# Layer 1's sixteen experts placed ahead of the shared expert in a four-layer kernel

## The chip, the cores and the metric

The kernel runs on one core of a Trainium2 chip. The metric is device time in microseconds for one launch; lower is better. A core has a matrix engine (PE, with its weight loads shown apart as PEld), a vector engine (DVE), a scalar engine (ACT), a general engine (POOL) and a queue engine (SP). Each works through its own instructions in the order in which they were laid down, and they meet through semaphores. SP issues the ordinary transfers of this kernel, POOL the indirect ones (rows scattered or gathered by a list of positions).

## The reference, cut to what matters

The program is a stack of four layers over x of shape 4 x 1024 x 128. Each layer has a mixing step and a feed-forward step, each added to x and followed by a layer norm. The change lies in layer 1's feed-forward step: 16 experts of width 128, of which every token takes four, and a shared expert of width 256 that every token takes.

```python
x = _layernorm(x + _L0_attn_ref(x, ...)); x = _layernorm(x + _L0_ffn_ref(x, ...))
x = _layernorm(x + _L1_attn_ref(x, ...)); x = _layernorm(x + _L1_ffn_ref(x, ...))
x = _layernorm(x + _L2_attn_ref(x, ...)); x = _layernorm(x + _L2_ffn_ref(x, ...))
x = _layernorm(x + _L3_attn_ref(x, ...)); x = _layernorm(x + _L3_ffn_ref(x, ...))

def _L1_ffn_ref(hidden_states, ...):          # layer 1's feed-forward step
    topk_idx, tw = _route(x, router_w, bias)  # 4 of 16 experts for each token
    combine = (one_hot(topk_idx, E) * tw[..., None]).sum(1)
    h = einsum('td,edf->etf', x, gate_w); u = einsum('td,edf->etf', x, up_w)
    y = einsum('etf,efd->etd', silu(h) * u, down_w)
    routed = einsum('etd,te->td', y, combine)
    sh = silu(x @ sh_gate_w) * (x @ sh_up_w) @ sh_down_w
    return routed + sh
```

Routed part and shared part are summed into the same rows of x before the norm, so they may be computed in either order.

## The kernel before, in words

All arithmetic is float32. x lies in on-chip memory as 32 tiles of 128 tokens; eight tiles are a quarter of the sequence positions. The first half is quarters 0 and 1 (part `a`), the second half quarters 2 and 3 (part `r` in layer 1). A transposed copy, `xT`, feeds the matrix multiplications.

Layer 1's experts are reached through lists in device memory. `spread` (L1305) scatters each row of x four times into the list `l1ra`, sorted by expert: 64 indirect transfers on POOL. `l1_experts` (`small_experts`, L1713 and following) works through the list in 18 groups of four tiles: SP loads a group's rows `xg` (L1336), PE turns them, multiplies by the gate and up weights (`gu`), ACT and DVE form `hg` (L1743, L1744), PE turns and multiplies by the down weights (`yp`), and SP stores the result `yg` to the list `l1ya` (L1762). Two further groups stand in a branch that is taken only when the lists are longer than that. `l1_close` then calls `collect`: POOL gathers the four rows of each token tile from `l1ya` into a tile `yt` (64 indirect transfers again, into a ring of five tiles), and DVE adds them with their weights to x (L1396, four instructions a tile). After eight tiles it norms the quarter, saves it (`xsave`) and turns it into `xT`.

`l1_shared` is the shared expert: for each of four blocks of 512 tokens four multiplications of 128x512 (`pg`, `pu`), SiLU on ACT (L743), a product on DVE (L744, `hs`), eight multiplications `py`, and one DVE addition to x (L830). Its weights are three loads of 128 KB (`swg`, `swu`, `swd`).

The second half runs as a companion: `side` is `l0_ffn` of quarters 2 and 3 (a quantised linear layer, DVE and POOL lines L487 to L544) and then `l1_attn` of quarters 2 and 3 (a state recurrence: L649 multiplies, L653 scans, L671 and L672 multiply back, L680 adds to x, then a norm by nine small DVE instructions and the eight of L212). `l2_weights` merges layer 2's weights in 24 steps, which start from the load `ld<-in_l_big` (1536 KB) and store through `we` (L1448, L1450).

The order is set by Python generators. `mix(main, side, pace)` advances the side by planned costs while the main generator is laid down; `chain` runs generators one after another, `abreast` side by side. The instructions are then ordered for each engine by a scheduler with priorities, and buffers of a pool that is closed are handed to the next pool, so that a load into a new pool waits for the last reader of the old one. The lines around the change are these:

```python
side = self.chain(self.l0_ffn((2, 3), True), self.l1_attn((2, 3), True))
self.run(self.mix(self.chain(self.l1_shared(a), self.l1_experts(a, wall)), side, 2.0, False))
self.run(self.mix(self.abreast(self.l2_weights(), side), self.l1_close(a, yp)))
```

After them come `l2_attn(0)`, which needs both quarters of the first half closed, and everything else.

Of the kernel before, what the change touches and what calls it, by code (L numbers as in the profile page):

```python
# [74 lines left out]
class Kernel:  # L75
# [737 lines left out]
    def l1_shared(self, part):  # L813

        nc, x = self.nc, self.x
        with ExitStack() as ctx:
            cp = self.pool(ctx, "l1sc" + part.name)
            hp = self.pool(ctx, "l1sh" + part.name, 2)
            ps = self.pool(ctx, "l1sp" + part.name, 2, space=PSUM)
            swg = self.load(cp, self.ins["l1_swg"])  # L820
            swu = self.load(cp, self.ins["l1_swu"])
            swd = self.load(cp, self.ins["l1_swd"])
            for blk in range(part.t0 // 4, (part.t0 + part.nt) // 4):
                h = self.tile(hp, [P, 2, BLK], "hs")
                for c in range(2):
                    f = slice(c * P, (c + 1) * P)
                    self.glu(ps, hp, h[:, c, :], swg[:, f], swu[:, f], blk)
                py = self.down(ps, h, swd, 2)
                tl = slice(blk * 4, blk * 4 + 4)
                nc.vector.tensor_tensor(x[:, tl, :], py, x[:, tl, :], ALU.add)  # L830
                yield (5.5,)

    def l1_close(self, part, yp):

        nc, x = self.nc, self.x
        for q in range(part.q0, part.q0 + part.nq):
            yield from self.collect("l1", part, K1, yp, (q - part.q0) * QT, QT)
            self.norm(self.quarter(q))
            tl = slice(q * QT, (q + 1) * QT)
            nc.sync.dma_start(out=self.xsave[:, tl, :], in_=x[:, tl, :])  # L840
            yield (6.0,)
            for g in range(2):
                self.turned(self.side, q * QT + g * 4, tag="s")
                yield (1.5,)
# [1037 lines left out]
    def all(self):  # L1882
        a, rest = self.first, self.rest
        b, c = rest
        r = self.both[1]
        a2, m2, n2 = self.by_rows
        with ExitStack() as ctx:
            lgp = self.pool(ctx, "l2lg")
            self.l2_lg = self.tile(lgp, [P, NT, E2], "lg")
            with ExitStack() as early:  # L1890

                self.l0_setup(early)
                self.l2_wr = self.load(lgp, self.ins["l2_wr"])
                self.run(self.l0_attn((0, 1)))
                self.l1_setup()
                self.l2_setup()
                self.zero_lists("l1")
                self.run(self.l0_ffn((0, 1)))
                self.run(self.l1_attn((0, 1)))

                self.run(self.l1_route(a))
                self.run(self.mix(self.l0_attn((2, 3), True), self.spread("l1", a, K1)))
                self.zero_lists("l2", "l3")
                with ExitStack() as c2:
                    wall = self.l1_wall(c2)
                    yp = self.pool(c2, "l1ya", 5, right=True)
                    side = self.chain(self.l0_ffn((2, 3), True), self.l1_attn((2, 3), True))
                    self.run(self.mix(self.chain(self.l1_shared(a), self.l1_experts(a, wall)), side, 2.0, False))
                    self.run(self.mix(self.abreast(self.l2_weights(), side), self.l1_close(a, yp)))
            with ExitStack() as c2:  # L1910
                wall = self.l1_wall(c2)
                self.run(self.mix(self.l2_attn(0), self.chain(self.l1_route(r), self.spread("l1", r, K1))))
                wall2 = self.l2_wall(c2)
                yp = self.pool(c2, "l1yr", 5, right=True)
                self.run(self.mix(self.chain(self.l1_experts(r, wall), self.l1_shared(r)), self.routed(a2)))
                self.run(self.mix(self.l2_experts(a2, wall2), self.l1_close(r, yp)))
            listed = lambda name: lambda: name in self.listed
            on = self.served(
                self.chain(self.rows_in(a2), self.onward(a, True)),
                (lambda: self.rows_done >= B + 2, self.routed(m2)),  # L1920
                (lambda: self.rows_done == 2 * B, self.routed(n2)),
            )
            self.run(self.mix(self.l2_attn(1), on, drain=False))
            with ExitStack() as c3:
                with ExitStack() as c2:
                    wall = self.l2_wall(c2)
                    self.press(on, listed("l2m"))
                    self.run(self.mix(self.l2_experts(m2, wall), on, drain=False))
                    self.press(on, lambda: {"l2n", "routed l3a"} <= self.listed)
                    sw, wall3 = self.l3_wall(c3, True)  # L1930
                    on = self.chain(on, self.rows_in(m2))
                    self.run(self.mix(self.l2_experts(n2, wall), on, drain=False))
                self.press(on, listed("l3a"))
                yp = self.pool(c3, "l3y", 8)

                on = self.chain(
                    on, self.collect("l2", n2, K2, yp, which=(0, 1, 4, 5)),
                    self.abreast(
                        self.chain(self.l3_attn(b), self.mark("mixed l3b"), self.l3_route(b)),
                        self.collect("l2", n2, K2, yp, which=(2, 3, 6, 7)),  # L1940
                    ),
                    self.abreast(
                        self.chain(self.spread("l3", b, K3), self.when(listed("made l3a")), self.last(a, yp)),
                        self.chain(self.l3_attn(c), self.mark("mixed l3c"), self.l3_route(c)),
                    ),
                    self.spread("l3", c, K3), self.when(listed("made l3b")), self.last(b, yp),
                )
                self.run(self.mix(self.chain(self.l3_shared(a, sw), self.l3_experts(a, wall3)), on, 0.75, False))
                hold = self.pool(c3, "l3hold", 2)
                for p in (b, c):  # L1950
                    self.press(on, listed("mixed l3" + p.name))
                    sh = self.tile(hold, [P, QT, D], "sh")
                    self.run(self.mix(self.l3_shared(p, sw, sh), on, 0.75, False))
                    self.press(on, listed("l3" + p.name))
                    self.run(self.mix(self.l3_experts(p, wall3), on, 0.75, p is c))
                    s = slice(p.t0, p.t0 + QT)
                    self.nc.vector.tensor_tensor(self.x[:, s, :], sh, self.x[:, s, :], ALU.add)
                self.run(self.close(c, yp))
        bad = self.nc.values_load(self.flag[0:1, 0:1], min_val=0, max_val=1)
        with self.tc.If(bad > 0):  # L1960
            with ExitStack() as ctx:
                lgp = self.pool(ctx, "l2lg2")
                self.l2_lg = self.tile(lgp, [P, NT, E2], "lg")
                self.l2_wr = self.load(lgp, self.ins["l2_wr"])
                self.l2_attn_general()
                for p in self.by_rows:
                    self.run(self.routed(p))
                    with ExitStack() as c2:
                        self.run(self.l2_experts(p, self.l2_wall(c2)))
                    self.run(self.rows_in(p))  # L1970
                for p in self.parts:
                    self.run(self.onward(p))
                    with ExitStack() as c2:
                        sw, wall = self.l3_wall(c2)
                        self.run(self.l3_shared(p, sw), self.l3_experts(p, wall))
                        self.run(self.last(p, self.pool(c2, "l3y" + p.name, 5)))
# [165 lines left out]
```

## Time and profile before

| What | Value |
|---|---|
| median of three timed runs | 2432.44 us (2420.16 to 2435.95) |
| the profiled execution | 2430.2 us, its span 2428.4 us |
| mean granted PE clock | 0.821 |
| PE, PEld busy | 1597.9 us, 952.6 us |
| DVE, ACT, POOL busy | 1272.6 us, 804.3 us, 780.6 us |

The span is the time from the first to the last instruction; 1.8 us of the profiled execution lie around it. No engine is busy all the time, so the program is a sequence of stages with limits of their own. The stages around the change, from the trace in us from the start of the span: the first shared multiplication at 399.70, the first expert multiplication at 433.76, the last stores to `l1ya` issued by 510.7, the first gather at 513.70, the last of L1396's additions of the first half at 633.26, and the first multiplication by layer 2's attention weights at 639.27.

### The profile page before, as it was taken

The numbers are of one execution on the slowest core, as the hardware profiler recorded it, in microseconds if no ns is written. First come the engines' busy times: TensorE is split into PE (matmuls) and PEld (weight loads), VectorE is DVE, ScalarE is ACT, GpSimd is POOL, SyncE is SP. The second block draws the span as 40 slices with busy tenths as digits, with TensorE's granted clock in tenths as the row PEclk, the third lists the DMA queues.
The fourth block names the chain that finished last, engine by engine and source line by source line (L and its number), as shares of the span: only waits on it lengthen the run. The fifth ranks groups of instructions, "written<-read, shape, count | busy, mean of one in ns | idle before, by whom it ended". The sixth has DMA issues, their size and how long they took to land. (4 is left out here: it accounts for less than half of the span.)

```text
span 2428.4 us, 27065 instructions
## 1 busy us (share of the span) xinstructions
PE 1597.9 (66%) x9017; PEld 952.6 (39%) x9017; DVE 1272.6 (52%) x3628; ACT 804.3 (33%) x1161; POOL 780.6 (32%) x701
## 2 busy tenths in 40 slices
PE   6535776866671675677969787887726798357160
PEld 2214433743330344544623232344414486145160
DVE  8767895655670564324535674573602265236233
ACT  5511372322330332212336554632201164223030
POOL 5531285145227002234132002002272200735724
PEclk9766788988785888888979998988867899679575
DMA  9930002334201014312130000031411131222232
GB/s 308 288 107 0 14 34 81 118 113 151 77 29 52 16 64 149 97 46 74 41 104 21 1 1 18 1 118 35 160 66 35 39 112 50 76 76 65 89 88 68
DMA packets 215531, 187.11 MB, mean 77 GB/s; under 512 B 16528, under 2 KB 194064, under 8 KB 214864
## 3 DMA queue, kind: packets, MB, share of 16 engines
q1 hardware_dynamic: 194672, 142.29, 18.5%
q0 software_dynamic: 20704, 42.86, 5.7%
q8 instruction: 84, 1.38, 0.2%
q14 instruction: 71, 0.58, 0.1%
HBM read 88.49 MB, written 96.60 MB: 76 GB/s over the span
## 5 line engine op out<-in xcount | busy, mean ns | idle before, releaser
L1059 ACT ACTIVATE pr<-sc 128x1024 f32<-128x1024 f32 x288 | 279.7, 1021 | 318.3 <-PE sc L157 189.2
L157 PE MATMUL gu<-ld,xgT 128*128 x640 | 173.4, 416 | 77.2 <-issue 39.2
L157 PE MATMUL sc<-qm,kT 32*128 32x512 f32 (+3 forms) x1536 | 200.3, 558 | 16.9 <-issue 9.7
L157 PE MATMUL s<-pr,va 128*32 128x512 f32 (+3 forms) x1536 | 173.9, 521 | 46.1 <-issue 26.3
L157 PEld LDWEIGHTS gu<-ld,xgT 128*128 128x128 f32 x640 | 125.5, 207 | 105.9 <-issue 50.0
L169 DVE COPY hT<-tp 128x512 f32<-128x512 f32 x118 | 81.0, 686 | 151.0 <-remote 75.8
L157 PE MATMUL gu<-wall,xgT 128*128 x304 | 156.2, 640 | 2.7 <-ACT xgT L167 2.0
L165 PE MATMUL tp<-ld,xg 128*128 128x128 f32 x396 | 67.2, 299 | 130.1 <-DMA xg<-l3rc 48.5
L165 PE MATMUL tp<-ld,hg 128*128 128x128 f32 x624 | 100.5, 282 | 77.0 <-issue 39.7
L1065 DVE TENSOR_TENSOR pr<-pr,ld 128x512 f32<-128x512 f32 (+1 forms) x160 | 92.3, 581 | 102.6 <-ACT pr L1059 96.5
L1744 DVE TENSOR_TENSOR hg<-sg,gu 128x256 f32<-128x256 f32 x160 | 65.7, 417 | 152.0 <-ACT sg L1743 104.2
L167 ACT COPY xgT<-tp 128x512 f32<-128x512 f32 x99 | 57.9, 586 | 243.5 <-PE tp L165 84.5
L157 PEld LDWEIGHTS sc<-qm,kT 32*128 32x128 f32 x1536 | 85.3, 196 | 117.2 <-issue 78.2
L165 PEld LDWEIGHTS tp<-ld,hg 128*128 128x128 f32 x624 | 79.3, 145 | 129.3 <-issue 74.1
L1743 ACT ACTIVATE sg<-gu 128x256 f32<-128x256 f32 x160 | 60.9, 385 | 166.4 <-PE gu L157 71.9
L1305 POOL DMA_INDIRECT l1ra<-x,posl1a x64 | 94.9, 1482 | 60.7 <-DVE posl1a L1280 41.5
L1502 ACT ACTIVATE sg<-gu 128x512 f32<-128x512 f32 x76 | 45.2, 597 | 206.5 <-PE gu L157 115.1
L1305 POOL DMA_INDIRECT yt<-l1yr,posl1r x64 | 60.7, 948 | 139.6 <-DVE x L1396 79.3
L165 PEld LDWEIGHTS tp<-ld,xg 128*128 128x128 f32 x396 | 50.3, 153 | 135.7 <-issue 83.7
L157 PEld LDWEIGHTS s<-pr,va 128*32 128x32 f32 x1536 | 38.6, 112 | 155.4 <-issue 108.0
L1305 POOL DMA_INDIRECT l1rr<-x,posl1r x64 | 62.5, 976 | 96.3 <-DVE posl1r L1280 77.1
L1305 POOL DMA_INDIRECT yt<-l1ya,posl1a x64 | 70.0, 1094 | 69.9 <-DVE x L1396 29.3
(444 smaller groups left out, 3505.8 us busy)
## 6 DMA issues: line engine op xcount, KB each, us to landing
wall<-wall SPq DMA_DIRECT2D x16, 768.0 KB
l3ra<-zero SPq DMA_DIRECT2D x1, 6144.0 KB
ld<-in_l_w SPq DMA_DIRECT2D x2, 3072.0 KB
wall<-we SPq DMA_DIRECT2D x24, 256.0 KB
ld<-in_l_w SPq DMA_DIRECT2D x1, 6144.0 KB
l1ra<-zero SPq DMA_DIRECT2D x1, 5120.0 KB
l1rr<-zero SPq DMA_DIRECT2D x1, 5120.0 KB
xg<-l3ra SPq DMA_DIRECT2D x20, 256.0 KB
```

The source lines that it names most:

```text
L157: return self.nc.tensor.matmul(out, lhsT, rhs, start=start, stop=stop)
L165: nc.tensor.transpose(pt[:, k * P : (k + 1) * P], s, self.ident)
L167: nc.scalar.copy(dst, pt[:, : n * P])
L169: nc.vector.tensor_copy(dst, pt[:, : n * P])
L1059: nc.scalar.activation(pr, sc[h], AF.Exp)
L1065: nc.vector.tensor_tensor(d, d, cst["tril"].unsqueeze(1).unsqueeze(1).to_broadcast([P, 2, n, P]), ALU.mult)
L1305: ins = self.nc.gpsimd.indirect_dma_start(**kw)
L1502: nc.scalar.activation(sg, gu[:, 0, :], AF.Silu)
L1743: nc.scalar.activation(sg, pg[:, :, 0, :], AF.Silu)
L1744: nc.vector.tensor_tensor(h[:, 2 * c : 2 * c + 2, :], sg, pg[:, :, 1, :], ALU.mult)
```

## The change

The experts of the first half are laid down first, with the second half's companion beside them as before. The shared expert is laid down afterwards, ahead of `l2_weights` and of what is left of the companion, with the gathers of `l1_close` as its side. A mark says that the shared expert has been laid down, and `l1_close` does not norm a quarter before that.

```diff
@@ l1_shared
                 nc.vector.tensor_tensor(x[:, tl, :], py, x[:, tl, :], ALU.add)
                 yield (5.5,)
+        self.listed.add("shared l1" + part.name)
 
@@ l1_close
             yield from self.collect("l1", part, K1, yp, (q - part.q0) * QT, QT)
+            yield from self.when(lambda: "shared l1" + part.name in self.listed)
             self.norm(self.quarter(q))
@@ all
                     side = self.chain(self.l0_ffn((2, 3), True), self.l1_attn((2, 3), True))
-                    self.run(self.mix(self.chain(self.l1_shared(a), self.l1_experts(a, wall)), side, 2.0, False))
-                    self.run(self.mix(self.abreast(self.l2_weights(), side), self.l1_close(a, yp)))
+                    self.run(self.mix(self.l1_experts(a, wall), side, 2.0, False))
+                    on = self.chain(self.l1_shared(a), self.abreast(self.l2_weights(), side))
+                    self.run(self.mix(on, self.l1_close(a, yp)))
```

The second half's layer 1 (part `r`) keeps its order: there the shared expert already follows the experts.

## The prediction

> **What bounds the kernel now.** I read the stages first (busy time by stretch), because shares over the whole span mix stages with different limits. Columns: us, busy us of PE, PEld, DVE, ACT and POOL, granted PE clock, DMA share, GB/s.
>
> ```profile
> core 0: us, PE busy (x) PEld busy (x) DVE busy (x) ACT busy (x) POOL busy (x), PEclk, DMA share, GB/s
> 399.70:433.80 34.10, 27.65 (x117) 16.95 (x117) 19.26 (x23) 6.04 (x11) 9.47 (x4) 0.90 0.08 24
> 433.80:513.70 79.90, 70.39 (x468) 62.72 (x468) 54.30 (x147) 31.53 (x67) 9.48 (x4) 0.99 0.38 112
> 513.70:528.70 15.00, 8.45 (x20) 3.64 (x20) 2.39 (x11) 3.79 (x9) 11.43 (x12) 0.70 0.48 173
> 528.70:557.20 28.50, 22.19 (x91) 12.96 (x90) 18.90 (x58) 7.31 (x17) 11.23 (x8) 0.94 0.29 101
> 557.20:582.60 25.40, 20.97 (x91) 12.03 (x90) 16.48 (x37) 7.84 (x18) 18.76 (x16) 1.00 0.49 153
> 582.60:610.70 28.10, 7.04 (x21) 3.64 (x21) 11.69 (x60) 3.13 (x7) 15.20 (x16) 0.65 0.49 164
> 610.70:633.60 22.90, 9.47 (x29) 4.30 (x27) 13.30 (x59) 5.21 (x9) 13.40 (x12) 0.72 0.38 119
> ```
>
> The rows are: shared expert, experts, wait for `ld<-in_l_big`, `l1_attn` of quarter 2, the first part of quarter 3, its second part, and the tail of gathers. PE fills the first two. After 513.70 no engine is full: instructions wait for one another.
>
> Then I read what SP waits for between 388 and 440 (columns: total, times, longest).
>
> ```profile
> SPq L1336 <- PE pu L157: 25.3, 1, 25.3
> ```
>
> The experts' first rows are not asked for until the shared expert's last `pu`, since they take over the buffers of its weights. Then the timeline: start, us, engine, line; in brackets the idle time before and what ended it.
>
> ```profile
> 512.03 0.34 SPq L153 DMA_DIRECT2D ld<-in_l_big  x1
> ...
> 513.70 1.02 POOL L1305 DMA_INDIRECT yt<-l1ya,posl1a  x1 [21.98 <-DMA l1ya<-yg]
> ...
> 518.92 1.19 PE L157 MATMUL s<-ld,ld 128*128 128x512 f32 x1 [9.25 <-DMA ld<-in_l_big]
> ...
> 528.66 1.29 DVE L649 TENSOR_TENSOR b<-s,wi 128x512 f32<-128x512 f32 x2 [12.57 <-issue]
> ...
> 559.25 0.94 POOL L1305 DMA_INDIRECT yt<-l1ya,posl1a  x1 [17.10 <-DVE x L1396]
> ...
> 614.86 0.94 POOL L1305 DMA_INDIRECT yt<-l1ya,posl1a  x1 [12.19 <-DVE x L1396]
> ```
>
> PE stands 9.25 us for the big load; DVE stands 12.57 us. POOL twice stops because `yt` has five tiles and DVE's additions, laid down behind `l1_attn`, have not freed one. So POOL is not the bound: the companion's chain is. Last, the timeline of DVE's `va` memsets (L911 to L913), first in this stretch, then at a place without gathers:
>
> ```profile
> 593.45 0.11 DVE L911 MEMSET va<- 128x64 f32 x1
> 595.38 0.17 DVE L177 TENSOR_SCALAR rstd<-rstd 128x8 int32<-128x8 int32 x1 [1.81 <-DVE va L911]
> ...
> 1218.77 0.43 DVE L912 MEMSET va<- 128x448 f32 x1
> 1219.16 0.11 DVE L913 MEMSET va<- 128x64 f32 x1
> ```
>
> Each of the twelve is followed by about 1.9 us of nothing between 587.2 and 608.5; at 1218 they run back to back.
>
> **The change, part by part.** Comparing the order on every engine, nothing is added or removed; the order differs only from 399.7 to the close of layer 1's first half. The wait added to `l1_close` costs nothing, because shared is always laid down before it is asked. So I walk to the last L1396 addition; before, it ends at 633.6.
>
> *Experts first.* The last `spread` has passed SP at 398.8; SP's queue then holds the row loads with nothing ahead. A load lands between 1.65 us (last gather's end 631.6 to its addition at 633.26) and 4.4 us (`xsave` issued 638.97, its reader at 643.4); I take 2.5, nearest the gather, which also reads list rows. Turning takes 1.4 (432.38 to 433.76): first expert multiplication at 402.8. PE then starts cold: the row of 0.90 clock over 34.1 us says 3.4 us are lost there; about half falls to the experts, 1.5. Gain 433.76 − 404.3 = 29.5.
>
> *The experts' own stage.* It now carries both `l0_ffn` chains of quarter 2, where before it carried about one and a half chains (quarter 3's cost some 3 us, the rest of quarter 2's 1.7). I take +2.5, between −1 (all hidden under PE, which is busy 70.39 of 79.90) and +6 (two chains of 3 us bare). First gather: 513.7 − 29.5 + 2.5 = 486.7.
>
> *Shared, beside the gathers.* Its three weight loads are issued on SP past the row loads and eighteen stores, in buffers the experts have just released: issue 485.0, landing 487.5 with the 2.5 above. It took 31.4 us (399.70 to the last L830 at 431.1), of which 3.8 and 2.8 were waits on `l0_ffn`, now elsewhere: 24.8. End: 512.3. Its eight SiLUs on ACT lie under PE. POOL's L503 (2.35 us) now stands before the first gather and L505 after the third; neither delays the end, since POOL had 17.10 and 12.19 us to spare.
>
> *The big load.* Its buffers now lie over shared's weights, and on SP it stands behind them: issue about 512, where before it was 512.03. It landed in 6.9 us; so first use 519, before 518.92. All 27 us gained so far are gone here: the experts' and shared's stages have only changed places, and the gathers hide beside shared instead of beside the rest.
>
> *Up to quarter 2's `l1_attn`.* Before, 518.92 to 528.66, 9.7 us. Now quarter 3's `l0_ffn` lies here too, which shared or experts used to hide: cold weights' pair 3.7, two blocks to 530, norm 7.9 (508.15 to 516.08), turning, weight triples and multiplication 6.5, so 544; a loss of about 15.
>
> *Quarter 2's `l1_attn`.* Row 528.70:557.20 is 28.5. Into it fall sixteen L1396 (0.272 apart, 4.4), norm 2.9, L212 2.15, reciprocal 0.2, four L959 1.6, a wait for `xsave` 2.2: 13.4, of which DVE's idle 9.6 (28.5 − 18.90) takes 7.5. So 34.4, to 578.4. Bounds: 32.3 (all 9.6 filled) and 41.9 (none).
>
> *Quarter 3's.* 557.2 to 610.7 was 53.5. Twenty-four additions leave (6.5). The memset stretch's excess is some 15 us (21.3 less about 6.5 free). The gathers that stood beside all twelve are mostly over by now; one tile's four (5 us) remain: excess 3.8, a saving of 11. So 36, to 614.4; with the excess wholly kept 47, wholly gone 32.2.
>
> *The tail.* Before 22.9 for sixteen gathers after L212. Now two tiles, eight gathers at 1.25 = 10, additions to free the ring 2.2, landing and last addition 2.6, less 0.7 of overlap: 14.1, ending 628.5. All behind it (closing norm, layer 2, rope and weights loaded by 617) moves alike.
>
> Sum: 628.5 − 633.6 = −5. Against the profiled execution's 2430.2 this is 2425; the median of the timed runs is 2.2 above that execution.
>
> A page speaks against the largest saving. In the Trainium skill, "SBUF — State Buffer", section "Who interferes with whom", a DVE instruction with at most one SBUF input, outside the two-port modes, does not contend with GpSimd, and a memset that does is named for trn3 alone. The rows show memsets delayed beside gathers and free without them, which is coincidence in one place and no proof. By the rows the stretch shrinks and the sum is −5; by the page its cause is elsewhere and the sum is about +6.
>
> **The rivals.**
>
> *The gathers set the end.* If the close follows the gathers' start, its 119.9 us (513.7 to 633.6) begin at 486.7 and end at 606.6: −27, 2403. For it: POOL starts 27 us earlier. Against it: POOL's stops of 17.10 and 12.19 us end on DVE's additions, which are queued behind the companion, and the companion starts with the big load, no earlier than before.
>
> *The memset stretch stays.* Between 577.94 and 593 a weight load of 3 MB fills the DMA engines; the stretch, 587 to 608, comes on its heels. In the changed order that load is issued at about 599 and the memsets come from 602, so the two coincide again. If this, not the gathers, delays each memset, the saving of 11 is lost: 628.5 + 11 = 639.5, +6, 2436. It decides from 5 us of kept excess on; below that the sum stays a gain. Against it: gathers ran throughout the slow stretch, also after 593, when DMA had thinned. If the experts' stage also goes to +6 and `l1_attn` of quarter 2 to 41.9, the same case reaches 2447.
>
> *Nothing is moved.* Excluded: the order comparison shows shared behind the experts on PE, DVE, ACT and SP.
>
> **How the numbers follow.** The forecast, 2425: chance 0.55; its own range 2408 to 2442, from the bounds above (experts' stage ±3.5, landing ±1.5, `l1_attn` −2 to +7.5, stretch −4 to +11). Gathers set the end, 2403: 0.2. The stretch stays, 2436 and upward: 0.25. The range 2396 to 2450 spans all three and leaves out about 2 in 10. One per cent, 24 us, is about what a measurement of this kernel can tell from no change: faster than 2408 takes most of the gather case and little of the forecast, 0.18; slower than 2457 needs the stretch case with several terms at their far ends, and what I have not seen, 0.13; within, 0.69.
>
> **What would show it.** Right: first expert multiplication near 404, first gather near 487, first use of `ld<-in_l_big` at 519 with PE idle before it, first L649 of quarter 2 near 544, the memsets mostly back to back, the last L1396 near 628. The prediction is wrong if the big load lands well before shared ends (then most of the 27 us stays), if the memsets still show 1.9 us behind each, or if quarter 3's `l0_ffn` between shared and `l1_attn` takes much over 25 us.

## The result

The changed kernel takes 2438.94 us (median of 20 runs) and the kernel before 2428.81 (20 runs): a ratio of 1.0043, 95% interval 1.0025 to 1.0062, some 10 us slower. The forecast was 2425, 5 us faster. The time lies in the forecast's range (2396 to 2450), but the change goes the other way.

The same program was met at two levels, and each ratio below is taken within one of them: the kernel before takes 2420 to 2430 us beside the changed kernel above and in the last four runs of the experiments, and 2074 to 2077 us in the other fourteen, with one chip showing both.

The stages of the changed kernel, by busy time (columns as in the prediction): experts, shared expert, big load to quarter 2's first L649, quarter 2's `l1_attn`, quarter 3's, tail of gathers.

```profile
core 0: us, PE busy (x) PEld busy (x) DVE busy (x) ACT busy (x) POOL busy (x), PEclk, DMA share, GB/s
402.90:484.30 81.40, 71.86 (x464) 63.47 (x464) 55.68 (x121) 33.04 (x68) 14.45 (x7) 0.96 0.40 116
484.30:530.20 45.90, 28.46 (x96) 17.03 (x96) 11.54 (x16) 4.78 (x8) 25.45 (x22) 0.76 0.11 29
530.20:559.00 28.80, 21.25 (x79) 11.80 (x80) 13.16 (x59) 10.05 (x23) 10.15 (x11) 0.88 0.42 146
559.00:601.80 42.80, 24.20 (x94) 15.11 (x94) 28.55 (x102) 8.97 (x19) 26.13 (x22) 0.76 0.28 92
601.80:634.00 32.20, 22.93 (x102) 13.80 (x100) 21.77 (x72) 8.56 (x18) 7.54 (x8) 0.92 0.52 191
634.00:645.00 11.00, 0.53 (x3) 0.18 (x1) 6.62 (x25) 0.71 (x2) 6.00 (x4) 0.50 0.34 120
```

The shared expert's row is the one to look at: 45.9 us for 28.46 us of PE, DVE busy 11.54, and POOL, with its gathers, busiest but for PE. The timeline of the changed kernel shows where the time lies idle (L1307 and L1398 here are L1305 and L1396 of before):

```profile
493.51 1.23 DVE L506 TENSOR_TENSOR qt<-qt,qt 128x1024 f32<-128x1024 f32 x1 [5.80 <-POOL qt L505]
...
514.63 0.94 POOL L1307 DMA_INDIRECT yt<-l1ya,posl1a  x1 [0.30 <-issue]
518.51 0.69 DVE L830 TENSOR_TENSOR x<-py,x 128x512 f32<-128x512 f32 x1 [12.78 <-remote]
518.59 0.60 ACT L743 ACTIVATE sg<-pg 128x512 f32<-128x512 f32 x1 [11.94 <-remote]
...
536.06 2.08 PE L157 MATMUL s<-ld,ld 128*128 128x512 f32 x2 [6.55 <-DMA ld<-in_l_big]
...
590.58 0.95 POOL L1307 DMA_INDIRECT yt<-l1ya,posl1a  x1 [0.30 <-issue]
594.16 0.69 DVE L680 TENSOR_TENSOR x<-s,x 128x512 f32<-128x512 f32 x1 [11.10 <-remote]
...
627.78 0.11 DVE L915 MEMSET va<- 128x64 f32 x1
627.92 0.17 DVE L176 TENSOR_SCALAR rstd<-ve 128x8 int32<-128x8 int32 x1
```

Three waits are new. DVE's L506 stands 5.80 us for POOL's L505, which is queued behind three gathers, and the shared expert's first product is queued behind L506. Then DVE and ACT stand together for 12.78 and 11.94 us, and again for 11.10 and 10.7 us, on something the view calls "remote": no instruction that it knows of ended just before them.

The trace's semaphore events tell what it was. An instruction that is done raises a semaphore by one (its increment), and whoever waits for it goes on. Most increments of PE here are recorded 0.01 us after the end of their instruction. But the multiplication that L830 waits for ended at 507.62, and its increment is recorded at 518.49, with three more of PE's in the same 0.13 us. The next such bundle is at 594.14, of multiplications that ended by 585.26. Both come 2.6 to 2.9 us after the last gather of a train (514.63 + 0.94 and 590.58 + 0.95) has left POOL; a train is a row of gathers with nothing between them. PE had worked; its word came late.

The `va` memsets, on the other hand, now run back to back (627.0 to 630.6), although gathers run beside them and the 3 MB weight load was issued just ahead of them, at 622.2.

### The profile page after: what moved, and what is told of

Its sections match the earlier page's. It is cut to its first block, busy times and chain, and to the rows that moved or that the text cites. A ratio compares the mean times of both kernels' runs of the same rounds, so it can differ in the third digit from the quotient of the medians.

```text
span 2433.1 us, 27068 instructions
## 1 busy us (share of the span) xinstructions
PE 1597.6 (66%) x9017; PEld 958.9 (39%) x9017; DVE 1274.5 (52%) x3628; ACT 803.9 (33%) x1161; POOL 779.0 (32%) x701
## 5 line engine op out<-in xcount | busy, mean ns | idle before, releaser
L1307 POOL DMA_INDIRECT l1ra<-x,posl1a x64 | 93.6, 1463 | 61.0 <-DVE posl1a L1282 41.8
L1307 POOL DMA_INDIRECT yt<-l1yr,posl1r x64 | 60.5, 945 | 139.3 <-DVE x L1398 78.2
L1307 POOL DMA_INDIRECT yt<-l1ya,posl1a x64 | 70.8, 1106 | 83.4 <-DVE x L1398 53.9
L1307 POOL DMA_INDIRECT l1rr<-x,posl1r x64 | 62.0, 968 | 99.0 <-DVE posl1r L1282 79.8
```

What stands on the lines that cost most here:

```text
L1307: ins = self.nc.gpsimd.indirect_dma_start(**kw)
```

## The experiments

Theory **trains**: while POOL issues gathers without a break, PE's increments, and later DVE's, are held until the train ends; the change has put two trains beside chains in which PE and DVE hand work to and fro. Rival **beside**: a gather next to such a chain slows it, trains or not. Rival **order**: the holes have nothing to do with POOL, and only the order on the engines counts.

### The first four, and the other level

**Breaks of 4 us after every eighth gather:**

```diff
+                sent += 1
+                if lay + part.name == "l1a" and sent % 8 == 0:
+                    self.pause(ins, 4)   # four memsets of 128x1024 on POOL, in order behind ins
```

> The changed kernel with four memsets of a scratch tile (about 4 us) on POOL after every eighth gather of layer 1's first half; the order on PE, DVE, ACT and SP is that of the changed kernel. Theory 'trains': when POOL issues gathers without a break, PE's semaphore increments are held until the train ends; in the changed kernel that holds the shared expert's second py from 507.6 to 518.5 and quarter 2's attention from 584.8 to 594.1. With breaks neither hold lasts over about 4 us: last L830 some 8 us earlier, quarter 2's second L680 some 8 us earlier again, the whole 10 to 18 us faster than the changed kernel, in spite of 28 us more work on POOL. Rival 'beside': any gather next to the shared expert slows it, however they are spaced: no gain, 0 to 5 us slower for the pauses in the tail. Rival 'order': the holes are not POOL's doing at all: no gain, 0 to 5 us slower.

Measured 2081.02 us, 1.0023 of the kernel before (1.0007 to 1.0038).

**A ring of eight tiles:** `yp = self.pool(c2, "l1ya", 8, right=True)`

> The changed kernel with a ring of eight yt tiles in place of five, so that the first train has 32 gathers and not 20 (POOL's order is unchanged; DVE's additions move a little). Theory 'trains': the hold of the shared expert lasts until this longer train ends, some 15 us more: last L830 near 545 in place of 530, the whole 8 to 15 us slower than the changed kernel. Rival 'beside': the same density of gathers, so the shared expert takes the same 46 us up to the train's old end and little more: 0 to 4 us. Rival 'order': 0, or up to 3 us faster because gathers run further ahead.

Measured 2075.49 us, 0.9995 (0.9978 to 1.0012).

**The first gather behind L505:** the name of L505's instruction is put on the list that the next indirect transfer is ordered behind.

> The changed kernel with the first gather held behind POOL's L505 of quarter 3, by an order on POOL alone; nothing else moves. The shared expert's first product L744 stands on DVE behind L506, which waits for L505: it should come at about 492.6 in place of 495.9. Theory 'trains': the train starts 3.6 us later without its break, PE is held all the same, until the train's end near 518: within 2 us of the changed kernel. Rival 'order': the 3.3 us are kept to the end: 3 us faster. Rival 'beside': 3 us faster as well.

Measured 2075.10 us, 0.9998 (0.9981 to 1.0014). The first product L744 comes at 492.43 in place of 495.09 (the changed kernel at this level, below) and the last L1398 ends at 619.1 in place of 621.6. The place and size are as expected where nothing is held, 2.5 us in the trace; it is too little for the ratio to show.

**The big load in buffers of its own:**

```diff
+                    self.l2wc = self.pool(c2, "l2wc")       # ahead of the shared expert's pools
             swd = self.load(cp, self.ins["l1_swd"])
+            if part.name == "a":
+                self.l2_in = self.load(self.l2wc, self.ins["l2_big"]), self.load(self.l2wc, self.ins["l2_ab"])
```

> The changed kernel with the 1536 KB load for layer 2's weights in buffers of its own below the shared expert's, issued on SP right behind the shared weights (near 483 in place of 529.5). All theories: the 6.55 us that PE waits for it after the shared expert go. If the companion's chain sets the end, as the prediction has it: 5 to 7 us faster than the changed kernel. If the gathers or the holds set it: 0 to 3 us. If 'trains' is right the holds at 507 to 518 and 584 to 594 stay, though the second may move.

Measured 2069.54 us, 0.9965 (0.9952 to 0.9979): 7 us below the kernel before, with which the changed kernel itself is level here (next section). The load is issued at 489.61, and PE no longer waits for it.

In these runs the kernel before took 2076.84 us. In their traces 2 of PE's some 1500 recorded increments come over 1 us late, and in the first two traces 90 of 1440 and 91 of 1449. So the first two of the four had nothing to act on and say nothing for or against the trains.

### Both kernels at the level without late increments

> The changed kernel itself once more, with the kernel before beside it. In the runs of the two kernels PE's semaphore increments came late during trains of gathers (held from 507.6 to 518.5 and from 584.8 to 594.1); in the traces of the runs since, hardly one was late, and the kernel before took 2076.84 us there. Theory 'trains' and the prediction's walk together: without holds the changed kernel's last L1398 should come some 20 us earlier than 645, near 621 to 626, and the change is worth what the walk says without the memset stretch's saving, -5 + 11, so 0 to +6 us against the kernel before. Rival: the loss of 10 us is the order's alone and is found again here: +8 to +12 us. If holds are there in this run, 645 and +10 us again.

Measured 2078.24 us, 1.0003 (0.9988 to 1.0018): no difference, and the rival's +8 to +12 is excluded here.

> The kernel before itself, for its trace beside the others. 'Trains': if no increments are held here, the twelve va memsets run back to back although gathers run beside them, and quarter 3's attention takes some 10 to 15 us less than 53.5. Rival 'memsets beside gathers': the 1.9 us behind each memset are found again.

Measured 2080.52 us, one run. The memsets of the kernel before, with gathers beside them:

```profile
587.54 0.95 POOL L1305 DMA_INDIRECT yt<-l1ya,posl1a  x1 [0.31 <-DMA yt<-l1ya,posl1a]
587.64 0.11 DVE L911 MEMSET va<- 128x64 f32 x1
587.82 0.43 DVE L912 MEMSET va<- 128x448 f32 x1
...
588.68 0.11 DVE L911 MEMSET va<- 128x64 f32 x1
...
588.79 0.94 POOL L1305 DMA_INDIRECT yt<-l1ya,posl1a  x1 [0.30 <-issue]
```

All twelve take from 587.6 to 591.2, 3.6 us where it was 20.4. In the Trainium skill, "SBUF — State Buffer", section "Who interferes with whom", a DVE instruction with at most one SBUF input, outside the two-port modes, does not contend with GpSimd; for these memsets, which read nothing, this trace agrees.

In the first trace of the kernel before, what stood between the memsets were the norm's small steps (L176 to L183), each of which needs the one before:

```profile
593.28 0.17 DVE L176 TENSOR_SCALAR rstd<-ve 128x8 int32<-128x8 int32 x1 [1.89 <-remote]
...
598.91 0.17 DVE L180 TENSOR_TENSOR nwt<-rstd 128x8 f32<-128x8 f32 x1 [2.90 <-remote]
```

L200, which L176 needs, ended at 591.40; between then and the start of L176 increments of DVE are recorded at 592.55 and 593.26 alone, up to 1.9 us late. So what delayed each step there was its increment; DVE's came one by one while the train still ran, not in a bundle behind it.

The two rows of the changed kernel that differ at this level, shared expert and quarter 2:

```profile
483.50:518.10 34.60, 26.96 (x96) 16.18 (x96) 11.72 (x16) 4.78 (x8) 25.43 (x22) 0.78 0.13 39
...
547.20:581.20 34.00, 24.72 (x96) 15.26 (x97) 28.58 (x102) 9.85 (x21) 26.13 (x22) 0.85 0.36 122
```

They are 11.3 and 8.8 us shorter than at the first level, 20.1 of the 22 us between the two walks from the first turned `xg` to the last addition (219.9 against 242.1). The granted clock alone does not set the levels apart: the experts' stage, which has no train beside it, takes 81.9 us at this level and 81.4 at the other, at a clock of 0.96 in both.

### Where the gain went

**More of the companion beside the experts:** `self.run(self.mix(self.l1_experts(a, wall), side, 1.5, False))`

> The changed kernel with the companion laid down faster beside the experts (pace 1.5 in place of 2.0), so that all of quarter 3's l0_ffn stands among the experts and none of it beside or behind the shared expert. The walk says that l0_ffn of quarter 3 between the big load and quarter 2's attention costs some 15 us, and L503 to L507 in the shared expert 4 to 8 us; against that the experts' stage grows by 3 to 6 us. So 12 to 20 us faster than the changed kernel. Rival 'gathers set the end': the gathers start no earlier, so 0 to 3 us.

Measured 2066.22 us, 0.9956 (0.994 to 0.9973) of the kernel before, and 12 us below the changed kernel's 2078.24: the lower end of the 12 to 20 expected. Its stages:

```profile
403.10:492.10 89.00, 76.41 (x488) 65.75 (x489) 64.00 (x149) 34.04 (x70) 18.96 (x8) 0.98 0.36 106
492.10:516.70 24.60, 23.18 (x96) 13.70 (x96) 11.95 (x30) 4.78 (x8) 18.42 (x20) 0.93 0.17 50
516.70:530.60 13.90, 7.48 (x19) 3.45 (x20) 2.11 (x9) 3.74 (x9) 8.09 (x9) 0.75 0.56 195
...
591.10:612.20 21.10, 7.33 (x20) 3.60 (x19) 11.32 (x47) 2.37 (x5) 13.55 (x12) 0.66 0.48 161
```

The shared expert falls to 24.6 us (the forecast's 24.8, now that nothing of `l0_ffn` is in it) and the way to quarter 2's L649 from 29.1 to 13.9. The experts grow by 7.1, and the tail from 11.0 to 21.1, since POOL now waits for a free `yt` tile until quarter 3's norm is over.

**The same, and the big load early:**

> As the last one, and the big load in buffers of its own as before (issued near 483). The two act at different places of one chain, so their gains add: another 6 to 7 us, 18 to 27 us faster than the changed kernel. If the gathers become the bound first (64 gathers at 1.25 us and their additions, from 487), less: their train alone would end near 570 and leaves room.

Measured 2057.12 us, 0.9904 (0.9872 to 0.9936): 21 us below the changed kernel, as expected.

**And a ring of eight:**

> The changed kernel with pace 1.5, the big load in its own buffers and a ring of eight yt tiles. In the last trace of pace 1.5 with the early big load POOL stood 16.88 us for a free yt tile behind quarter 3's L212 and then had twelve gathers to do, so that the last addition came 21 us after that L212. With eight tiles those twelve gathers are done before: if the ring is what the tail waits for, the tail shrinks to some 6 to 9 us, 10 to 15 us faster than with five tiles. Rival 'gathers set the end': POOL has no time to spare for them, 0 to 3 us. If increments are held behind long trains here, a longer train is slower: the tail's gain is lost again.

Measured 2051.12 us, 0.9884 (0.9862 to 0.9907). The tail shrinks from 20.9 to 11.9 us, less than to the 6 to 9 expected, and quarter 3 ends 2.8 us later; the ratio can't be told from the one without the longer ring, so the 10 to 15 us were not found. All three versions with the faster companion beat both kernels at this level; at the other they were not run.

**The kernel before with breaks, and with a ring of eight:**

> The kernel before with four POOL memsets (about 4 us) after every eighth gather of layer 1's first half. Theory 'trains', where increments are held behind trains (twelve va memsets from 587.2 to 607.6 in the first trace): the breaks release them, the memsets take under 10 us, the whole is 5 to 15 us faster than the kernel before. Where nothing is held (va from 587.6 to 591.2): the pauses only lengthen the tail of gathers, 4 to 10 us slower.

Measured 2088.89 us, 1.0064 (1.0041 to 1.0087): with nothing held, the breaks only cost, 13 us and not 4 to 10.

> The kernel before with a ring of eight yt tiles alone. Its tail from quarter 3's L212 to the last addition is some 23 to 30 us for sixteen gathers that wait for the ring. If the ring is the wait: twelve of these gathers move ahead of the L212, 8 to 14 us faster. Then a part of what the change was to bring by starting the gathers earlier is to be had without it. Rival 'gathers set the end': 0. Where increments are held behind trains, the longer train holds DVE longer and eats the gain.

Measured 2069.37 us, 0.9984 (0.9967 to 1.0000): some 3 us in place of 8 to 14. The tail after quarter 3's L212 is still 31 us, and from 568.2 on POOL gathers without a stop (32 gathers at some 1.25 us and a few longer ones), so the ring is not what it waits for: the gathers themselves fill it.

The breaks once more:

> The changed kernel with the breaks on POOL once more, in case the kernel before takes 2429 us beside it and not 2075 (the two levels seen so far). At 2429, theory 'trains': no PE increment is held over about 4 us, 10 to 18 us faster than the changed kernel's 2439, so 2421 to 2429; rival 'beside': 2439 to 2444. At 2075 nothing is held and the run can only repeat the first one: 2078 to 2085.

Measured 2081.00 us, 1.0033 (1.0006 to 1.0061), at the 2075 level.

### Delays put in by hand

If nothing is held, PE can be kept busy at the places of the holds.

```diff
-        self.mm(pg, wg, self.xT[:, c])
+        for _ in range(1 + again):       # 26, in the shared expert's second block
+            self.mm(pg, wg, self.xT[:, c])
```

> The changed kernel with PE kept busy at the two places where its increments were held in the changed kernel's first trace: one multiplication of the shared expert's second block (pg) is repeated 26 times (26 x 0.43 = 11.2 us; that stage took 45.9 us where held and 34.6 where not) and one of quarter 2's attention (L649's input) 20 times (8.6 us; 42.8 and 34.0). Each repeat writes the same values again, and the order on every engine is that of the changed kernel. Theory 'holds on the path': both delays reach the last L1398 in full, so 18 to 21 us over the 2076 to 2078 of the changed kernel, 2094 to 2099. Rival 'slack': POOL and DVE catch up behind, 5 to 12 us.

> The kernel before with PE kept busy in quarter 2's attention (12 repeats, 5.2 us) and in quarter 3's (37 repeats, 15.9 us), the places and sizes of its own holds (28.4 against 23.1 us, 53.5 against 37.5 us). Theory: 21 us of delay, of which the tail gives some 7 back, because POOL goes on gathering meanwhile (the tail after quarter 3's L212 was 22.9 us where held and 29.8 where not): 13 to 17 us over the kernel before, 2088 to 2092. With the other run this makes the changed kernel 3 to 8 us the slower of the two, as in the first measurement (10 us), though without these delays they are equal. Rival 'no slack': 19 to 21 us, and no difference between the two.

Measured 2114.15 us, 1.0194 (1.0169 to 1.0219), and 2113.36 us, 1.0185 (1.0160 to 1.0211). A repeat is two records of 0.43 us, so the delays were twice what was meant: 39.6 us make 37 in the changed kernel and 42.1 make 37 in the kernel before. Nearly all of a delay at these places reaches the end in both; "slack" falls, and in the kernel before the tail gave nothing back (29.7 us). The next pair was to have the right sizes and, for the kernel before, the place of its hold:

> As the run of the changed kernel with repeats, with half of them: a multiplication turned out to be two records of 0.43 us, so 13 repeats are 11.2 us in the shared expert and 10 are 8.6 us in quarter 2's attention, the sizes of the two holds. In the last run 39.6 us of repeats made 37.3 us. 'Holds on the path': 18 to 19 us over the changed kernel's 2077, 2095 to 2096. 'Slack': 5 to 12 us.

> The kernel before with 6 repeats of quarter 2's multiplication (5.2 us) and, at the place where DVE was held (the norm of quarter 3, among the va memsets), 64 repeats of one bn_stats (L192, 0.25 us each, the same values again: 16 us). In the last run of the kernel before the delay stood ahead of the additions of L1396, and the tail gave nothing back (29.7 us). Here the additions are done and POOL's ring is free when the delay comes. If the place is what lets the tail give some 7 us back (22.9 us in the first trace): 13 to 15 us over the kernel before's 2076, 2089 to 2091, and so 4 to 7 us less than the changed kernel with its delays. If not: 18 to 19 us, and the two kernels are equal again.

Here the kernel before was back at 2419.94 us, with 90 late increments of PE in each of the two traces. Measured 2440.40 us, 1.0079 (1.0059 to 1.0100), and 2444.56 us, 1.0102 (1.0078 to 1.0125). As a pair they don't answer their question, since hand-made and real delays stand in them together: the repeats in the shared expert took the place of its hold (49.6 us in all, no "remote" wait), and quarter 2's hold stayed.

### Breaking the trains where increments are late

> The changed kernel with breaks of about 4 us on POOL after every eighth gather of layer 1's first half, at the level of the first measurement if it is still there (the kernel before took 2420 us in the last two runs and increments came late again). Theory 'trains': with at most eight gathers on end no increment waits beyond a break; no hold near 507 to 518 or 584 to 594; last L830 some 8 us earlier than 530, last L1398 near 628 to 634 in place of 645, 10 to 16 us faster than the changed kernel (1.0043 of the kernel before), so 0.998 to 1.000 of it. Rival 'beside': late increments come with any gather: holds as before, 1.004 to 1.007. At the 2075 level it repeats 1.0023 to 1.0033.

Measured 2423.93 us beside 2429.08: 0.9980 (0.9954 to 1.0005), where the changed kernel without breaks, which was not run again beside it, is at 1.0043. The first and the third of the shared expert's four L830 in this run:

```profile
506.12 0.69 DVE L830 TENSOR_TENSOR x<-py,x 128x512 f32<-128x512 f32 x1 [4.99 <-PE py L157]
...
518.41 3.99 POOL L1323 MEMSET rest<- 128x1024 f32 x4
520.14 0.69 DVE L830 TENSOR_TENSOR x<-py,x 128x512 f32<-128x512 f32 x1 [5.23 <-PE pu L157]
```

The long wait is gone. What is left of it stands before the third: its multiplication ended at 516.79, and the increment comes in a bundle at 520.12, 1.7 us into a break and 3.3 us late. (The view names `pu` here and not "remote", because another multiplication had ended shortly before.) No "remote" wait is left between 380 and 680, and from the first turned `xg` to the last L1398 it takes 226.3 us in place of 242.1.

> The kernel before with the same breaks, at the same level. Theory 'trains': the twelve va memsets, which took from 587.2 to 607.6, are no longer held: under 8 us in all; quarter 3 gains 12 to 15 us, the pauses cost some 13 us in the tail (1.0064 where nothing was held): 0.999 to 1.003 of the kernel before. Rival 'beside': memsets held as before and the pauses on top, 1.006 to 1.01. At the 2075 level it repeats 1.0064.

Measured 2425.45 us: 0.9981 (0.9961 to 1.0000), a little better than the 0.999 to 1.003 forecast. The memsets of this run are all done in 4.4 us (592.6 to 597.0), with gathers beside them:

```profile
592.57 0.95 POOL L1305 DMA_INDIRECT yt<-l1ya,posl1a  x1 [0.30 <-issue]
592.62 0.11 DVE L911 MEMSET va<- 128x64 f32 x1
...
596.01 4.03 POOL L1321 MEMSET rest<- 128x1024 f32 x4
596.91 0.11 DVE L913 MEMSET va<- 128x64 f32 x1
```

So the trains are shown to be the cause of the long holds: breaks alone, with more work on POOL and no other instruction moved on PE, ACT or SP, shorten them to a few us or take them away in both kernels. "Beside" and "order" fall. With breaks the two kernels are equal (0.9980 and 0.9981), as they are where nothing is held. Why a train holds increments at all, and at one level alone, no run here shows.

## Why the prediction was wrong, step by step

| Mark, us | forecast | changed kernel | the same, nothing held |
|---|---|---|---|
| first gather | 486.7 | 486.60 | 485.78 |
| first shared multiplication | 487.5 | 484.34 | 483.52 |
| last L830 ends | 512.3 | 530.24 | 518.14 |
| first use of the big load | 519 | 536.06 | 523.99 |
| first L649 of quarter 2 | 544 | 559.04 | 547.23 |
| quarter 2's L212 ends | 578.4 | 601.8 | 581.2 |
| quarter 3's L212 ends | 614.4 | 634.0 | 610.6 |
| last L1398 ends | 628.5 | 645.03 | 621.6 |

The first gather is right to 0.1 us, partly by luck: the first expert multiplication came at 404.75 and not at 402.8, and from there to the first gather it took 81.9 us where the walk has 83.9, so two errors of 2 us cancel. The walk's main point is right too: the experts' and shared's stages change places, the big load comes no earlier, and the 27 us are gone by its first use. The pace and the early load, which give 21 us back where nothing is held, show where most of them went.

*Shared, beside the gathers: 24.8.* This is the step that failed. It measured 45.9, 21.1 us more. Of these 9.8 are there with nothing held (34.6), and most of them, 7.8, are L505's: the forecast looked at POOL's own slack and found none harmed, but DVE's L506 waits for L505, and the shared expert's first product stands behind L506 (11.6 us after the first multiplication; 3.8 before). With all of `l0_ffn` out of the way it is 24.6. The other part, 11.3 us, is the held increments, for which the forecast has no term.

*The big load, and up to quarter 2's `l1_attn`: 6.9 and 25.* The load took 6.5 us to its first use, and from there it was 23.0.

*Quarter 2's `l1_attn`: 34.4.* Without a hold it is 34.0. With it, 42.8: the second place where held increments, which the sum lacks, were lost time.

*Quarter 3's, a saving of 11.* The saving came (32.2 us against a forecast of 36), and the memsets run free. But its cause was misread: not that gathers stand beside memsets, but that DVE's increments come late towards the end of a train. Where nothing is held the kernel before has no such stretch (37.5 us in place of 53.5) and there is nothing to save. The same misreading hid that this cost would follow the gathers to wherever they were put.

*The tail: 14.1.* It was 11.0.

*The rivals.* "The gathers set the end" is refuted: POOL stands 26.98 us for DVE ahead of 618.50. "The memset stretch stays" has the right sign, and with 2436 nearly the time, by luck: the 3 MB load fell beside the memsets as this rival has it, and they ran free. The time was lost in the shared expert, whose end came 17.9 us after its mark, and in quarter 2, which took 8.4 us too long.

How the 10 us divide: from the first turned `xg` to the last addition the holds cost the changed kernel 22 us (242.1 against 219.9) and the kernel before 15 (201.1 against 185.8), 7 of the 10. In the kernel before, the two stages with holds lost 21 us (28.5 against 23.2 and 53.5 against 37.5), but its tail was 7 shorter (22.9 against 29.8): POOL went on gathering while DVE was held. In the changed kernel nothing was given back. That reading of the tail was not confirmed by a run of its own. The remaining 3 us stay unassigned. The breaks, which take 15 us off the changed kernel and 5 off the kernel before, don't settle it, since they have prices of their own (some 4 to 6 and 13 us where nothing is held). Without holds the change is worth nothing that can be measured.

## What to carry to other kernels

Where a trace calls a wait "remote" and two engines end it at once, compare the end of the producing instruction with the time of its increment before you blame an engine. Where increments come late, a long unbroken train of indirect transfers belongs beside work that seldom hands over between engines, and a few breaks in it can be worth more than the place: here they took 15 us off the changed kernel, and cost 4 to 13 us where nothing was held. And when a step moves, ask for each queue it passes not only whether that engine has slack but who waits for what is now queued behind it.

## What the runs showed of the hardware

At the level of the first measurement, in the traces of the two kernels, take the trains of six and more gathers with at most 0.6 us between two, and call an increment late when it is recorded over 0.6 us after the end of the last instruction of its engine that raises this semaphore. Of PE's increments recorded while a train runs, 10 of 90 are late during its gathers 1 to 4, 10 of 45 at 5 to 8, 8 of 20 at 9 to 12 and 17 of 23 at 13 to 20; of DVE's 2 of 366 up to gather 20 and 10 of 30 behind it; of ACT's none of 81. In the two traces of the other level none of 516 of PE's is. Many increments wait until the train is over and come in a bundle, 2.6, 2.9 and 4.0 us after the last gather has left POOL in the first half of layer 1; others come late while it still runs.

Scatters hold increments too, and longer. In the kernel before, 64 of them leave POOL in one train from 708.72 to 790.4, and ACT stands for most of that time, until 5.9 us behind it:

```profile
796.33 1.02 ACT L1059 ACTIVATE pr<-sc 128x1024 f32<-128x1024 f32 x1 [68.50 <-remote]
```

Over the whole program DVE or ACT stands in waits called "remote" for 435 us of the kernel before and 403 us of the changed kernel, and in the traces of the other level not once. The whole program is 350 us longer at this level, so late increments are large enough to make up the difference; that they do, and what breaks in all the other trains would bring, was not tested. These traces also hold fewer semaphore records (1440 of PE's against 1494, and 392 against 1285 of one semaphore of POOL's indirect transfers).

What sets the level is open: the same kernel on the same chip was met at both, some fifty minutes apart. No run here tells whether the recording of the trace takes part in it.
